# A layer of 64 experts returns its results by one-hot products in PSUM in place of scatter-adds in DRAM

## The chip, the cores and the metric

The kernel is one launch on one core of a Trainium2 chip. The metric is the device time of that launch in microseconds (us). The core has the engines PE (matrix products; PEld is its weight load, which overlaps PE), DVE (vector), ACT (scalar functions), POOL (general, and the issuer of indirect transfers) and SP (issues plain transfers). Each takes its instructions in order and waits on semaphores for the others.

## The reference

A macaron network of four kinds of block over x of 16 × 256 tokens × 128 features in float32: x + half a feed-forward part, x + attention, x + half a feed-forward part again. The change lies in the feed-forward part of block 1, which runs twice, before and after that block's attention. It is a mixture of 64 experts. Each token goes to its best 8, but an expert takes 64 rows at most, the first 64 in token order. One shared expert takes all tokens.

```python
logits = x @ router_w.T
probs = softmax(logits)
topk_w, topk_ids = top_k(probs, 8)
topk_w = topk_w / sum(topk_w)
pos = position of the token in its expert's list, in token order
valid = pos < 64
h = silu(xb[e] @ w_gate[e]) * (xb[e] @ w_up[e])      # xb[e]: the 64 rows of expert e
y = h @ w_down[e]
routed = segment_sum(y[slot] * topk_w * valid, token)
return routed + silu(x @ ws_gate) * (x @ ws_up) @ ws_down
```

The layer around it is x = x + 0.5 · ffn(layernorm(x)).

## The kernel before

x stays in SBUF as 32 tiles of 128 tokens. `norm_piece(c)` normalises the four tiles of piece c (statistics and roots on DVE, then ACT), and `turn_piece(c)` transposes them with PE into `xnT`. Twelve steps run one after the other; block 1 is `ffn1(0, normed=False)`, `attn1()`, `ffn1(1, normed=True)`, and block 2 begins with `ffn2(0)`, whose choice of tokens (`pick`, `best`, `choose`) is begun inside the second `ffn1`.

Since an expert takes the first 64 of its tokens, and the inputs fill all lists from the first 1024 tokens, the common path looks at FIRST = 8 tiles alone. A count `more` of unfilled slots is read into a register on every engine (`values_load`, L1107), and a branch (L1108) runs the general path over all 4096 tokens when it is above zero. That path is not taken with these inputs.

`ffn1` has three stages:

1. Routing (L985 to L1070): logits on PE, the best eight per token on DVE, then `slots` turns the keys and takes the first 64 per expert with eight rounds of max and replace on DVE. This gives `idx`, the token of each of the 64 × 64 slots, and `idy`, the same for the scatter. The rows of an instruction hold a pair of experts, 2 × 64 slots, so 32 columns. At its end the shared expert handles the first two pieces (`shared_up`: gate product L970, up product L972, silu, product L975; `shared_down`: L981 and the addition to x, L983), and `store_x` writes the 8 tiles of x to the first of four accumulators in DRAM. The scheduler moves these instructions up into pauses of the routing, since they hang on nothing later.
2. A loop of 8 groups of 8 experts (4 pairs), a pipeline written out by hand: `pin` chains the instructions of an engine in program order. `fetch(g)` gathers a group's rows with four indirect transfers issued by POOL (L1121), `turn(g)` transposes them, `gates(g)` makes gate and up products (L1143), `product(g)` multiplies on DVE (L1150), `down(g)` makes y (L1159), scales it to `ys` on DVE (L1175), and scatters it: four indirect transfers that add rows of `ys` to an accumulator in DRAM (L1179). Successive pairs use different tensors, and the two experts of a pair different halves of one, so four accumulators in all. Between these stand, for six of the groups, the shared expert of one later piece, and the normalising and turning of pieces. The weights of group g+2 are loaded by SP after `down(g)`.
3. The return. The 8 tiles of x are read from the first accumulator and three more are added to them: in the first call by `returned` and `summed` inside `attn1` (L1349 to L1359), in the second by `gather_acc` (L939) ahead of `choose(range(2))`. For this the three other accumulators are filled with zeros on entry (L957).

[...] The loop's own pool holds hg, hu, the gate product `sg` (which yp shares), the up product `su`, and two of y; a pool of two banks, `pst`, with the one tag "tp", serves all transposes.

The order of a step g of the loop, first call: `fetch(g+3)`, `down(g)`, weights of g+2, `turn_piece`, `norm_piece`, `gates(g+1)`, `product(g+1)`, `shared_up`, `turn(g+2)`, `shared_down`. The second call has `pick` and `best` at the end of a step besides; `best` is a row of max, find and replace operations on DVE.

## Time and profile before

| what | value |
| --- | --- |
| nine runs, median (lowest to highest) | 2895.14 us (2884.4 to 2908.34) |
| the profiled execution: time, span, granted clock | 2898.89 us, 2897.2 us, 0.844 |
| `ffn1(0)`: routing; loop, first y to the next stage's first product | from 666; 727.68 to 813.50 us |
| `ffn1(1)`: loop, first y; last `best` in the loop ends | 985.66; 1112.98 us |
| scatter-adds on POOL (L1179) | 64, mean 1569 ns |
| gathers on POOL (L1121) | 64, mean 964 ns |
| fills of accumulators, all steps | 14 of 512 KB |
| loads of accumulators into `acc_t`, all steps | 28 of 256 KB |

The times come from one profiled execution. A group of instructions is named by line, engine, operation and tile (digits dropped, so `f_ys` is f1_ys and `acc` any of the four), the shape as partitions × elements, a count, busy time and mean of one, then the idle time of the engine ahead of them and what ended it. A line of a timeline has start, length, engine, source line, operation, tiles, shape and count, and in square brackets the idle time ahead of it with its releaser. The granted clock is that of TensorE as a share of full speed.

### The profile page before, as it was taken

Reading aid. Unit: us, or ns where it says so; the run is one execution under the profiler, and the core shown is the slowest. Engines: PE = TensorE matmul, PEld = TensorE weight load, DVE = VectorE, ACT = ScalarE, POOL = GpSimd, SP = SyncE. Lnnn points to the kernel's source line nnn. Section 1 sums busy time; section 2 is a strip of 40 time slices with the busy share of each in tenths; the row PEclk is TensorE's granted clock in tenths of the full one; section 3 lists DMA queues with packets and bytes.
Section 4 is the critical chain, followed back from the end, with each engine's and each line's share of the span. In section 5 each row is a group of like instructions: output and inputs, shape, how many; then the busy total and the mean of one; then the engine's idle time right before and its main releaser. Section 6 shows DMA issues by size and latency. Waiting matters only on the chain. (4 is left out here: it accounts for less than half of the span.)

```text
span 2897.2 us, 45476 instructions
## 1 busy us (share of the span) xinstructions
PE 2324.3 (80%) x16717; PEld 1703.3 (59%) x16717; DVE 1489.3 (51%) x4376; ACT 1059.9 (37%) x2385; POOL 767.3 (26%) x695
## 2 busy tenths in 40 slices
PE   5976986993865573587999992776999899999999
PEld 4874554881655452354666661554777555557777
DVE  5446665445567556422345566124555566645453
ACT  1322221231334221343444432343444355553443
POOL 1650000561730452475000102772111100002111
PEclk9998886895769665555999995778999799989999
DMA  5861232563630445365000003552000012210000
GB/s 152 277 161 48 79 101 65 167 174 92 150 63 11 124 100 142 83 150 133 28 5 8 5 8 95 136 141 65 1 1 1 13 56 63 67 52 6 8 8 11
DMA packets 207909, 221.14 MB, mean 76 GB/s; under 512 B 46265, under 2 KB 172938, under 8 KB 204306
## 3 DMA queue, kind: packets, MB, share of 16 engines
q1 hardware_dynamic: 171066, 179.80, 20.2%
q0 software_dynamic: 36608, 38.31, 7.9%
q8 instruction: 135, 2.21, 0.3%
q14 instruction: 100, 0.82, 0.1%
HBM read 145.88 MB, written 63.50 MB: 72 GB/s over the span
## 5 line engine op out<-in xcount | busy, mean ns | idle before, releaser
L318 ACT ACTIVATE xn<-x,ln_less,ln_r 128x128 f32<-128x128 f32 x288 | 118.6, 482 | 376.0 <-DVE ln_less L309 347.3
L858 DVE TENSOR_REDUCE a_nm<-a_s 128x4 f32<-128x1024 f32 x128 | 156.4, 1224 | 101.0 <-PE a_t L854 89.8
L1652 PE MATMUL f_h<-f_xgT,f_w 128*128 128x128 f32 x768 | 161.8, 376 | 36.9 <-DVE f_xgT L1646 36.9
L503 PE MATMUL f_h<-f_xsT,f_w 128*128 128x256 f32 x736 | 183.6, 394 | 1.7 <-DVE f_xsT L492 1.7
L862 ACT ACTIVATE a_e<-a_t 128x512 f32<-128x512 f32 x256 | 139.1, 594 | 103.8 <-PE a_t L854 103.8
L854 PE MATMUL a_t<-a_q,a_k 32*128 32x256 f32 x1024 | 173.2, 424 | 4.7 <-ACT a_e L862 4.6
L1656 ACT ACTIVATE f_hs<-f_h,w_f_b 128x128 f32<-128x128 f32 x384 | 109.8, 368 | 182.2 <-PE f_h L1652 178.5
L1652 PEld LDWEIGHTS f_h<-f_xgT,f_w 128*128 128x128 f32 x768 | 137.7, 269 | 61.7 <-DVE f_xgT L1646 60.3
L1687 POOL DMA_INDIRECT acc<-f_ys,f_idx x96 | 151.8, 1581 | 55.9 <-DVE f_ys L1682 29.5
L506 DVE SCALAR_TENSOR_TENSOR f_hs<-f_h,f_b1s,f_sg 128x256 f32<-128x256 f32 x184 | 88.9, 484 | 141.9 <-ACT f_sg L505 140.7
L854 PE MATMUL a_s<-a_k,a_q 32*128 32x256 f32 x1024 | 154.7, 429 | 2.3 <-DVE a_nm L858 1.6
L505 ACT ACTIVATE f_sg<-f_h,f_b1s 128x256 f32<-128x256 f32 x184 | 87.1, 474 | 168.9 <-PE f_h L503 168.9
L503 PEld LDWEIGHTS f_h<-f_xsT,f_w 128*128 128x128 f32 x736 | 133.4, 196 | 24.6 <-issue 7.8
L326 PE MATMUL ln_tp<-ident,xn 128*128 128x128 f32 x288 | 64.2, 337 | 98.0 <-ACT xn L318 97.5
L1682 DVE TENSOR_SCALAR f_ys<-f_up,f_xg,f_share 128x128 f32<-128x128 f32 x96 | 39.4, 410 | 197.2 <-PE f_up L1679 163.4
L2072 ACT ACTIVATE f_nh<-f_c,w_f_sh 128x256 f32<-128x256 f32 x192 | 87.0, 500 | 127.7 <-DVE f_c L2091 103.2
L477 POOL DMA_INDIRECT f_xs<-xn_dram,f_src x92 | 90.7, 986 | 135.3 <-DVE f_own L446 60.6
L2019 POOL TENSOR_TENSOR f_t<-f_nh 128x512 f32<-128x512 f32 x16 | 20.3, 1272 | 380.8 <-PE f_m L2053 361.2
L854 PEld LDWEIGHTS a_t<-a_q,a_k 32*128 32x128 f32 x1024 | 107.0, 195 | 20.7 <-ACT a_e L862 14.2
L854 PEld LDWEIGHTS a_s<-a_k,a_q 32*128 32x128 f32 x1024 | 90.8, 197 | 46.9 <-issue 33.6
L1179 POOL DMA_INDIRECT acc<-f_ys,f_idy x64 | 100.4, 1569 | 65.5 <-DVE f_ys L1175 36.0
L326 PEld LDWEIGHTS ln_tp<-ident,xn 128*128 128x128 f32 x288 | 40.4, 162 | 125.3 <-ACT xn L318 111.3
(453 smaller groups left out, 5501.2 us busy)
## 6 DMA issues: line engine op xcount, KB each, us to landing
f_w<-in_f_w SPq DMA_DIRECT2D x24, 1024.0 KB
f_w<-in_f_w SPq DMA_DIRECT2D x46, 512.0 KB
f_w<-in_f_w SPq DMA_DIRECT2D x70, 256.0 KB
a_ud<-a_u SPq DMA_DIRECT2D x32, 512.0 KB
f_wgu<-in_f_wgu SPq DMA_DIRECT2D x16, 768.0 KB
acc<-zeros SPq DMA_DIRECT2D x14, 512.0 KB
acc_t<-acc SPq DMA_DIRECT2D x28, 256.0 KB
f_wd<-in_f_wd SPq DMA_DIRECT2D x16, 384.0 KB
```

What stands on the lines that cost most here:

```text
L318: S.activation(xn[:, t0 + j, :], x[:, t0 + j, :], AF.Identity, bias=less[:, j : j + 1], scale=r[:, j : j + 1])
L326: pin(PE.transpose(tp[:, i * P : (i + 1) * P], xn[:, 4 * c + i, :], ident))
L477: G.indirect_dma_start(out=xs[:, i, :], out_offset=None, in_=xn_dram, in_offset=bass.IndirectOffsetOnAxis(ap=src[:, s : s + 1], axis=0),)
L503: pin(PE.matmul(h[:, k, :], w1[:, cc * P : (cc + 1) * P], xsT, start=True, stop=True))
L506: V.scalar_tensor_tensor(hs[:, c, :], h[:, 1, :], b1[:, b, c : c + 1], sg, ALU.add, ALU.mult)
L854: pin(PE.matmul(ps[:, c, :], sta[:, c * P : (c + 1) * P], mov, start=True, stop=True))
L858: pin(V.tensor_reduce(m, sp, AX.X, ALU.max, negate=True))
L862: pin(S.activation(e, tp, AF.Exp, scale=scale))
L1179: G.indirect_dma_start(out=acc_two[e % 2], out_offset=bass.IndirectOffsetOnAxis(ap=idy[:, e : e + 1], axis=0), in_=ys[:, i, :], in_offset= ...
L1652: pin(PE.matmul(h[:, s, :], w1[:, e % GE2, s, :], xgT, start=True, stop=True))
L1656: pin(S.activation(acts[e][:, s, :], h[:, s, :], AF.Gelu, bias=W["f2_b1"][:, col : col + 1]))
L1687: G.indirect_dma_start(out=acc2[e % 2], out_offset=bass.IndirectOffsetOnAxis(ap=idx[:, e : e + 1], axis=0), in_=ys, in_offset=None, comput ...
```

## The change

The routed results of the common path no longer go through DRAM. For each pair e of experts and each half k of the 1024 tokens a one-hot matrix of 128 slots × 512 tokens is made by comparing a row of counting numbers with the slot's token (`tokf[:, k, e]`), on DVE for k = 0 and on POOL for k = 1 (`places`). PE multiplies: `sums[k] += ysᵀ · onehot` over all 32 pairs, in two PSUM banks that stay open through the loop (`put`). At the end ACT copies the two sums over the first 1024 columns of `xnT`, and `summed(c)` turns them back with four transposes and adds them to x.

The accumulators, `idy`, `store_x`, the fills and the loads go from the common path. Two banks for the sums are found by giving y one bank for two and by moving `sup`, the up product, into the pool of the transposes, in the routing stage as well. Every group's `ys` is stored to a new DRAM tensor `ys_dram` by SP; the general path alone reads it, and does its scatter-adds from there (its mending). `choose` takes the pieces two at a time, which is the same for the two pieces that the common path gives it.

```diff
+    ys_dram = dram.tile([E1 // 2 * P, D], F32, name="ys_dram")
...
+    def summed(c):
+        tp = pst.tile([P, 512], F32, tag="tp", name="f1_stp")
+        for i in range(4):
+            pin(PE.transpose(tp[:, i * P : (i + 1) * P], tok(4 * c + i), ident))
+        xc = x[:, 4 * c : 4 * c + 4, :]
+        pin(V.tensor_tensor(xc, xc, tp.rearrange("p (j d) -> p j d", d=D), ALU.add))
...
-        for a in acc[1:]:
-            zero_rows(a, 0, FIRST)
...
-                sup = pool.tile([F1, 512], F32, tag="su", name="f1_sup", bufs=1)
+                sup = pst.tile([P, 512], F32, tag="tp", name="f1_sup")[:F1, :]
...
-                    V.tensor_scalar(idy[rows, :], empty[rows, h::2], float(T + h * (T + PAD)), None, ALU.add)
+                    for k in range(2):
+                        V.tensor_scalar(tokf[rows, k, :], empty[rows, h::2], float(T - 512 * k), None, ALU.add)
...
-                store_x(acc[0], 0, FIRST)
...
+                count_up = op.tile([P, 512], F32, name="f1_no", bufs=1)
+                G.iota(count_up, pattern=[[1, 512]], base=0, channel_multiplier=0, allow_small_or_imprecise_dtypes=True)
+                sums = [ph.tile([P, 512], F32, name=f"f1_sum{k}") for k in range(2)]
+                def places(g):
+                    for i in range(n):
+                        e = g * n + i
+                        for k, eng in enumerate((V, G)):
+                            t = op.tile([P, 512], F32, tag=f"oh{k}", name="f1_oh")
+                            pin(eng.tensor_scalar(t, count_up, tokf[:, k, e : e + 1], None, ALU.is_equal))
+                            ohs[e, k] = t
+                def put(g):
+                    ys = yss.pop(g)
+                    for i in range(n):
+                        e = g * n + i
+                        for k in range(2):
+                            pin(PE.matmul(sums[k], ys[:, i, :], ohs.pop((e, k)),
+                                    start=e == 0, stop=e == E1 // 2 - 1, skip_group_check=True))
...
-                    y = ph.tile([P, n, D], F32, tag="y", name="f1_y", bufs=2)
+                    y = ph.tile([P, n, D], F32, tag="y", name="f1_y", bufs=1)
...
-                    for i in range(n):
-                        e = g * n + i
-                        pin(G.indirect_dma_start(out=acc_two[e % 2], ..., in_=ys[:, i, :], compute_op=ALU.add))
+                    SP.dma_start(
+                        out=ys_dram[g * n * P : (g + 1) * n * P, :].rearrange("(i p) d -> p i d", p=P), in_=ys)
...
                     if 1 <= g < groups - 3:
                         fetch(g + 3)
+                    places(g)
                     down(g)
...
                     if g + 2 < groups:
                         turn(g + 2)
+                    put(g)
                     if other:
                         shared_down(c, ph, sh, pin)
...
+                for k in range(2):
+                    pin(S.copy(xnT[:, k * 512 : (k + 1) * 512], sums[k]))
                 if normed:
                     best(first + others - 1, 2)
...
-                gather_acc(acc, 0, FIRST, n=4, bufs=6)
+                for c in range(FIRST // 4):
+                    summed(c)
                 choose(range(FIRST // 4))
...
-            for c in range(FIRST // 4):
-                returned(c)
...
-                    summed(piece_order[ahead[s]])
+                    if piece_order[ahead[s]] < FIRST // 4:
+                        summed(piece_order[ahead[s]])
```

`tokf` is a float tile of 128 × 2 × 32 in place of `idy`. The one-hots have four buffers for each half, which is one group's. `returned` and the old `summed` of `attn1` go.

More of the change, by code (lines that the diff above doesn't have):

```diff
@@ L962, in ffn1 @@
             idx = rp.tile([P, E1 // 2], I32, name="f1_idx")
-            idy = rp.tile([P, E1 // 2], I32, name="f1_idy")
+            tokf = rp.tile([P, 2, E1 // 2], F32, name="f1_tokf")
             more = rp.tile([1, 1], I32, name="f1_more")
@@ L1085, in general @@
                     )
-                    for a in acc:
-                        zero_rows(a, FIRST, NT)
+                    for a in acc[:2]:
+                        zero_rows(a)
                     key = key_pool.tile([P, NT // 2, 2, E1], F32, name="f1_gkey")
@@ L1111, in ffn1 @@
             pinned.clear()
-            with tc.tile_pool(name=f"f1h{call}", bufs=1, space=PSUM) as ph:
+            with tc.tile_pool(name=f"f1h{call}", bufs=1, space=PSUM) as ph, tc.tile_pool(
+                name=f"f1o{call}", bufs=GE1 // 2
+            ) as op:
                 n, groups, others = GE1 // 2, E1 // GE1, NT // 4 - FIRST // 4
-                xgs, turned, hidden, w = {}, {}, {}, early
+                xgs, turned, hidden, w, yss = {}, {}, {}, early, {}
+                count_up = op.tile([P, 512], F32, name="f1_no", bufs=1)
[13 more added lines that the diff above has]
+                        for k in range(2):
+                            pin(
+                                PE.matmul(
+                                    sums[k],
+                                    ys[:, i, :],
+                                    ohs.pop((e, k)),
+                                    start=e == 0,
+                                    stop=e == E1 // 2 - 1,
+                                    skip_group_check=True,
+                                )
+                            )
+                ohs = {}
                 def fetch(g):
@@ L1169, in down @@
                     flat = xgs.pop(g).rearrange("p e w -> p (e w)")
-                    ys = tp2.tile([P, n, D], F32, tag="ys", name="f1_ys", bufs=2)
+                    ys = yss[g] = tp2.tile([P, n, D], F32, tag="ys", name="f1_ys", bufs=2)
                     for h in range(2):
@@ L1175, in down @@
                         pin(V.tensor_tensor(ys[rows, :, :], y[rows, :, :], bc(wcol, 2, D), ALU.mult))
-                    for i in range(n):
-                        e = g * n + i
-                        pin(
-                            G.indirect_dma_start(
-                                out=acc_two[e % 2],
-                                out_offset=bass.IndirectOffsetOnAxis(ap=idy[:, e : e + 1], axis=0),
-                                in_=ys[:, i, :],
-                                in_offset=None,
-                                compute_op=ALU.add,
-                            )
-                        )
+                    SP.dma_start(
+                        out=ys_dram[g * n * P : (g + 1) * n * P, :].rearrange("(i p) d -> p i d", p=P), in_=ys
+                    )
                 first = FIRST // 4
@@ L1240, in ffn1 @@
             with tc.If(rv > 0):
-                gather_acc(acc, FIRST, NT, add=True)
+                with tc.tile_pool(name=f"f1s{call}", bufs=2) as sp2:
+                    idy = sp2.tile([P, E1 // 2], I32, name="f1_idy", bufs=1)
+                    for h in range(2):
+                        rows = slice(h * CAP1, (h + 1) * CAP1)
+                        V.tensor_scalar(idy[rows, :], tokf[rows, 0, :], float(h * (T + PAD)), None, ALU.add)
+                    for e in range(E1 // 2):
+                        ys = sp2.tile([P, D], F32, tag="ys", name="f1_gys")
+                        SP.dma_start(out=ys, in_=ys_dram[e * P : (e + 1) * P, :])
+                        G.indirect_dma_start(
+                            out=acc_two[0],
+                            out_offset=bass.IndirectOffsetOnAxis(ap=idy[:, e : e + 1], axis=0),
+                            in_=ys,
+                            in_offset=None,
+                            compute_op=ALU.add,
+                        )
+                gather_acc(acc[:2], FIRST, NT, add=True)
                 if normed:
@@ L1343, in norm @@
                 G.tensor_tensor(xc, xc, bc(W["a1_bo"], 1, 4), ALU.add)
-            def returned(c):
-                rows = slice(4 * c * P, (4 * c + 4) * P)
-                xc = x[:, 4 * c : 4 * c + 4, :]
-                SP.dma_start(out=xc, in_=acc[0][rows, :].rearrange("(j p) d -> p j d", p=P))
-                parts[c] = []
-                for a in acc[1:]:
-                    t = ap.tile([P, 4, D], F32, tag="acc", name="acc_t", bufs=6)
-                    SP.dma_start(out=t, in_=a[rows, :].rearrange("(j p) d -> p j d", p=P))
-                    parts[c].append(t)
-            def summed(c):
-                xc = x[:, 4 * c : 4 * c + 4, :]
-                for t in parts.pop(c, []):
-                    pin(V.tensor_tensor(xc, xc, t, ALU.add))
             pinned.clear()
-            parts = {}
-            for c in range(FIRST // 4):
-                returned(c)
             for c in begun:
@@ L1452, in choose @@
     def choose(cs):
-        for step in (norm_piece, turn_piece, pick, best):
-            for c in cs:
-                step(c)
+        for i in range(0, len(cs), 2):
+            for step in (norm_piece, turn_piece, pick, best):
+                for c in cs[i : i + 2]:
+                    step(c)
     def ffn2(call):
```

## The prediction

> **What bounds the kernel now.** I read the page's utilisation rows first, then the windows of the two expert loops, then their timelines and what ended each wait. The chain of waits reaches back only to 1797 us and says nothing of these loops.

> ```profile
> span 2897.2 us, 45476 instructions
> PE 2324.3 (80%) x16717; PEld 1703.3 (59%) x16717; DVE 1489.3 (51%) x4376; ACT 1059.9 (37%) x2385; POOL 767.3 (26%) x695
> 751.40:775.20 23.80, 20.04 (x139) 15.94 (x138) 13.48 (x52) 7.56 (x16) 18.37 (x16) 0.79 0.63 150
> 1034.00:1104.00 70.00, 49.13 (x270) 38.77 (x271) 43.73 (x161) 15.82 (x38) 29.37 (x21) 0.65 0.33 61
> ```

> The last two lines are windows (bounds, length, then busy time of PE, PEld, DVE, ACT, POOL, the granted clock, DMA share, GB/s). In loop 1 (first call, 727.7 to 813.5) two steps take 23.80 us and PE is busy for 20.04: TensorE has 3.8 us free in two steps. In loop 2 it has 21 of 70 free.

> ```profile
> 764.01 1.09 PE L1159 MATMUL f_y<-f_wd,f_hh 96*64 96x128 f32 x16
> 768.22 1.05 PE L970 MATMUL f_sgp<-xnT,w_f_sgu 128*96 128x512 f32 x2
> 769.10 1.02 PE L972 MATMUL f_sup<-xnT,w_f_sgu 128*96 128x512 f32 x2
> 769.96 0.60 PE L1132 MATMUL f_xtp<-ident,f_xg 128*128 128x128 f32 x4
> 773.91 1.34 PE L981 MATMUL f_yp<-w_f_sd,f_sh 96*128 96x128 f32 x8 [3.34 <-DVE f_sh L975]
> 775.18 1.98 PE L1159 MATMUL f_y<-f_wd,f_hh 96*64 96x128 f32 x16
> 783.06 1.97 PE L970 MATMUL f_sgp<-xnT,w_f_sgu 128*96 128x512 f32 x2
> 784.82 1.11 PE L972 MATMUL f_sup<-xnT,w_f_sgu 128*96 128x512 f32 x2
> ...
> 1040.49 2.07 PE L981 MATMUL f_yp<-w_f_sd,f_sh 96*128 96x128 f32 x8 [9.16 <-DVE f_sh L975]
> 1060.97 1.45 PE L981 MATMUL f_yp<-w_f_sd,f_sh 96*128 96x128 f32 x7 [4.64 <-DVE f_sh L975]
> ```

> Here a step lasts from one f_y to the next: 764.01 to 775.18 is 11.17 us at full clock with 3.34 idle, the next (775.18 to 787.86) 12.68 at a partly slow clock with 0.41 idle. A 128x512 f32 product costs 0.88 from start to start (768.22 to 769.10), 1.76 when slow (783.06 to 784.82). Loop 2 is paced by DVE and ACT; its step takes some 20 us.

> **Removed.** Per call: 32 scatter-adds on POOL, three 512 KB fills, the store and eight 256 KB loads of the accumulators, six DVE additions of 0.69.

> ```profile
> L1179 POOL DMA_INDIRECT acc<-f_ys,f_idy x64 | 100.4, 1569 | 65.5 <-DVE f_ys L1175 36.0
> ...
> 823.65 0.37 ACT L1282 COPY a_v<-a_vp 128x256 f32<-128x256 f32 x1 [10.24 <-DMA x<-acc]
> 824.07 1.22 PE L1276 MATMUL a_vp<-w_a_wv,xnT 128*128 128x128 f32 x4 [5.94 <-ACT a_v L1282]
> 1123.96 1.42 DVE L943 TENSOR_TENSOR x<-x,acc_t 128x512 f32<-128x512 f32 x2 [10.98 <-DMA acc_t<-acc]
> 1133.87 1.25 PE L326 MATMUL ln_tp<-ident,xn 128*128 128x128 f32 x3 [28.35 <-ACT xn L318]
> ```

> The scatters keep POOL busy but do not hold TensorE. On the path lie the waits after the loops: 10.24 on ACT, of which PE loses 5.94 at 824.07, and 10.98 on DVE in call 2. Loads, stores and fills are otherwise under the loops.

> **Added.** (1) PE: eight f32 products of 128x512 per group, 8 × 0.87 = 7.0 us at full clock, 14.1 slow; eight groups, two calls: 111 to 225 us. (2) Sixty-four one-hots a call, half on DVE and half on POOL. For DVE no 128x512 comparison is shown; the nearest rows are

> ```profile
> L190 DVE TENSOR_SCALAR same<-same,rowg 128x128 f32<-128x128 f32 x1 | 0.3, 255 | 0.0
> L1544 DVE TENSOR_SCALAR f_taken<-f_cv,f_lim 128x256 f32<-128x256 f32 x2 | 0.7, 343 | 0.0
> L2020 POOL TENSOR_TENSOR f_t<-f_nh 128x512 f32<-128x512 f32 x16 | 20.3, 1268 | 0.0
> ```

> from which 88 ns for 128 more columns gives 343 + 2 × 88 = 0.52; bounds 0.34 (half the width) and 0.69 (the 128x512 product of two tensors at L983). Four per group: 2.1 us (1.4 to 2.8). For POOL I take L2020's 1.27 (bounds 0.45, a fill of 128x2048 at 1.80 divided by four, and 1.58, the same L2020 with another input): with four gathers of 1.25 a step is 4 × 1.25 + 4 × 1.27 = 10.1 us, under PE's, so hidden; it would show if PE's step fell below that. (3) A 256 KB store of ys per group on SP. It waits there for ys, and behind it stand the weights of the group after next (768 + 384 KB). These wait for y of this group anyway, ys ends 1.4 later, and they are used a step later; at the 150 GB/s of the window they take 7.7 us of that step's 14: cost nothing, and what the step lacks if the cover is gone. (4) An iota on POOL ahead of the first gather, some 0.5 (rows of 0.23 for 128x128), and two ACT copies of the sums at the loop's end, some 0.7 each from the row of 0.37 for 128x256. (5) Four transposes and one addition in place of three additions.

> **Loop 1.** All of PE's step at full clock: y 1.02, turn_piece .50, gates 1.33 + 1.36, shared gate .88, up .86, turn .50, put 7.0, yp .9 = 14.3 us against a mean of 11.94. The wait of 3.34 is where put falls (it stands between turn and yp), but it is there only in every second step; the rest of put is added. DVE's step is 7.3 busy + 2.1 and with its waits 12 to 12.6: below 14.3. That is +2.4 a step. The last put (7.0) stands bare behind y(7), where no shared product or wait covers it, and so does the copy of the sums (0.8), which frees the bank that attention wants. At the end the wait for the accumulators goes: a_v stood 10.2 behind the loop's end (813.50) for their sake, and now follows the last put by about 2.4, the time of its own products and copy. The additions shrink from 5.2 (rows of 2.13 and 3.08 at 831.23 and 838.76) to 1.4, which with the transposes leaves −3.3.

> **The routing stage, a move that the diff hardly shows.** The up product of the shared expert now takes a bank of the pool that holds the transposes. In instruction order it so lands behind the key transposes, the list transpose and the count: the two shared chunks, before done between 670 and 685 (932 and 955 in call 2) inside routing's waits on DVE, now run after f_cp. The work: two ups 2 × 1.85, yp 2.0, addition .69, gate 1.97, silu .6, product .69, yp 2.1, addition .69 = 12.4 us in a row at the slow clock that PE has after such a pause. Routing itself ends some 3 us sooner without this work and the second index list (f_more 708.61 to 705.9), so DVE is free at 718.0 instead of 708.8. What is queued behind it on DVE is the branch:

> ```profile
> 712.95 0.87 DVE L295 BATCH_NORM_STATS2 ln_st<-x 128x6 f32<-128x128 f32 x4 [4.20 <-DVEq L1108]
> ```

> If the 4.20 follows the late end, norm_piece runs 722.2 to 726.3, xn to 728, the copy of the turned tokens after it on ACT, and the first gates start at 728.7 instead of 721.45: +7.3. If the branch is short (ACT shows 0.65 between its two neighbours in call 2), it is +3.8. Call 2 has no norm_piece there: +2.7, lower bound −0.8. I take the long one, since it is the same engine's row.

> **Sum of call 1.** y(0) 734.9, y(1) 753, five steps of 14.4 to y(6) 825, last put done 846.5, a_v at 848.9 against 823.65: +25.3; −3.3 for the additions: **+22**. **Call 2.** y(1) to y(3) come 8.2, 10.2, 11.6 late (these steps are PE's), then 0.4 to 2.1 each, the one-hots in DVE's chain; about +15 at y(6). After it the saved wait of 10.98 and the additions meet the last put, which delays pick and the last best by 7 (14.6 slow): −3.3 to +2.2. **+15** (+7 to +18). Together +37 on 2898.89 is 2936; the profiled run lies 3.75 above the median of nine, so 2932 on the median; forecast **2933**.

> [...] In loop 2 PE's granted clock is 0.65, in loop 1 0.79, and after a wait of 3.3 us the next products are slow for some 10 us. [...]

> **Rivals.** (A) PE stays slow in the loops: each put 14.1 instead of 7.0. For it: loop 2's 0.65. Against: the gaps that slow it in loop 1 are filled. All sixteen would be +112; for half of them +45 more: 2965 to 3040. (B) The one-hots become the bound, DVE and POOL holding each other up: a step of 16.5 instead of 14.3 is +15 in loop 1 and as much in loop 2: 2950 to 2965. For it: POOL's L2020 shows 1.27 and 1.58 for one shape, so POOL's time does stretch. Against: 14.3 leaves it 4 us. (C) Other side: POOL sets the pace now. Its step is 4 × 1.87 for scatters + 4 × 1.25 = 12.5 us, above the mean of 11.94, and it holds ys and the gathers; with 7.5 less, and with PE's 5.94 + 28.35 of tail idle to put the products into, both calls would shrink by some 10: 2875. It decides if PE's idle time per step is at least put's 7.0; the window shows 1.9 per step in loop 1 (10 in loop 2 but not in steps 0 to 3). (D) The shared work is hidden as before and the branch is short: that is 7 less on the sum, and with both tails at their good ends 8 less again: 2918.

> **Chances.** Forecast with its bounds (2915 to 2948) 0.50; D 0.15; B 0.12; A 0.10; C 0.07; no visible change, where D's gains and C's meet, 0.06. A measurement of this kernel tells about 0.3% (9 us) from no change. Slower by more: 0.87, within 0.06, faster 0.07. The range leaves out C and the upper A: 2907 to 2972.

> **What would show it.** After: f_y to f_y about 14.3 in loop 1 with a clock above 0.9 and no wait for f_sh (right), or steps above 16 with waits for f_oh on PE (B), or products of 1.76 (A). The shared ups after f_cp and hg(0) some 7 us later show the move; no idle DMA wait before a_v and before the summed additions shows the gain. The forecast is wrong if y's step stays near 12, or if PE waits for the xg gathers.

## The result and the profile after

The changed kernel takes 2950.53 us (median of 14 runs) against 2896.82 for the kernel before: a ratio of 1.0183, 95% interval 1.0167 to 1.0200, or +53.7 us. It is slower, as forecast, inside the stated range, and by half as much again as the +37 of the sum. The profiled execution has a span of 2945.7 us.

First two rows of the page, then two windows of the changed kernel, laid out as before (bounds, length, busy time of PE, PEld, DVE, ACT, POOL, clock, DMA share, GB/s): loop 1 from y(0) to y(7), and loop 2 from y(2) to y(7).

```profile
span 2945.7 us, 46050 instructions
...
PE 2397.8 (81%) x16989; PEld 1716.5 (58%) x16989; DVE 1521.6 (52%) x4436; ACT 1064.1 (36%) x2391; POOL 769.6 (26%) x697
```

```profile
731.81:829.44 97.63, 97.63 (x574) 61.82 (x573) 64.78 (x210) 25.29 (x55) 69.51 (x52) 0.99 0.38 115
1040.02:1149.64 109.62, 83.49 (x465) 52.11 (x464) 62.70 (x222) 19.90 (x46) 42.60 (x31) 0.89 0.22 68
```

Before the change loop 2 from y(2) to y(7) was this, and in its step from 1024.78 to 1045.44 the transposes of the gathered rows did not wait (the 9.16 us of idle time stood behind them, ahead of f_yp at 1040.49):

```profile
1010.24:1098.80 88.56, 65.29 (x386) 51.89 (x385) 53.75 (x205) 19.60 (x46) 46.48 (x35) 0.69 0.44 90
...
1030.73 0.60 PE L1132 MATMUL f_xtp<-ident,f_xg 128*128 128x128 f32 x4
```

In loop 1 PE is now busy for all of 97.63 us at a clock of 0.99. In loop 2 it is busy for 83 of 110: it has 26 us free, against 23 before, though 7 us of products were added to each step. One step of each, from the timeline of PE:

```profile
761.23 1.09 PE L1200 MATMUL f_y<-f_wd,f_hh 96*64 96x128 f32 x16
...
767.18 0.60 PE L1173 MATMUL f_xtp<-ident,f_xg 128*128 128x128 f32 x4
767.62 7.03 PE L1145 MATMUL f_sum<-f_oh,f_ys 128*128 128x512 f32 x16
774.49 1.06 PE L989 MATMUL f_yp<-w_f_sd,f_sh 96*128 96x128 f32 x8
775.47 1.09 PE L1200 MATMUL f_y<-f_wd,f_hh 96*64 96x128 f32 x16
...
1067.98 1.02 PE L980 MATMUL f_sup<-xnT,w_f_sgu 128*96 128x512 f32 x2
1075.32 1.12 PE L1173 MATMUL f_xtp<-ident,f_xg 128*128 128x128 f32 x4 [6.32 <-ACT xnT L328]
1076.23 8.12 PE L1145 MATMUL f_sum<-f_oh,f_ys 128*128 128x512 f32 x16
1084.18 1.06 PE L989 MATMUL f_yp<-w_f_sd,f_sh 96*128 96x128 f32 x8
1086.79 1.09 PE L1200 MATMUL f_y<-f_wd,f_hh 96*64 96x128 f32 x16
```

The step of loop 1 is 14.24 us (761.23 to 775.47) and has no gap. That of loop 2 (1062.88 to 1086.79) is 23.9 in place of 20.7 (1024.78 to 1045.44), and it has one gap: the transposes of the gathered rows wait 6.32 us for ACT to copy `xnT` out of a transpose bank, and the products, which stand behind them, are not even started. This wait is new.

The routing stage of the first call, as PE, then DVE and POOL saw it:

```profile
701.19 0.19 PE L1076 MATMUL f_cp<-ones,f_count 128*1 128x1 f32 x2 [1.42 <-DVE f_count L1074]
701.31 3.73 PE L980 MATMUL f_sup<-xnT,w_f_sgu 128*96 128x512 f32 x4
...
707.40 1.10 PE L978 MATMUL f_sgp<-xnT,w_f_sgu 128*96 128x512 f32 x2 [0.78 <-DVE x L991]
709.90 2.08 PE L989 MATMUL f_yp<-w_f_sd,f_sh 96*128 96x128 f32 x8 [1.40 <-DVE f_sh L983]
...
716.46 0.87 DVE L296 BATCH_NORM_STATS2 ln_st<-x 128x6 f32<-128x128 f32 x4 [3.75 <-DVEq L1116]
...
716.59 0.56 POOL L1126 IOTA f_no<- 128x512 f32 x1 [65.77 <-DVEq L1116]
```

The shared expert's products stand behind the count, as the instruction order said; DVE ends them at 712.71, and the branch takes 3.75 more. POOL, which has nothing to do with that work, starts its iota and so the first gathers only then (716.59).

The ends of both loops, ACT and DVE:

```profile
840.58 0.59 ACT L1274 COPY xnT<-f_sum 128x512 f32<-128x512 f32 x1 [8.83 <-PE f_sum L1145]
843.87 0.37 ACT L1336 COPY a_v<-a_vp 128x256 f32<-128x256 f32 x1 [1.84 <-PE a_vp L1330]
...
1169.79 0.43 DVE L1480 MAX8 f_cv<-f_lg 128x8 f32<-128x256 f32 x1 [9.32 <-ACT f_lg L1471]
1179.45 0.74 DVE L1774 TENSOR_SCALAR a_spread<-ones,rowm 128x64 f32<-128x64 f32 x4 [3.65 <-DMA f_w<-in_f_w]
```

The wait of a_v for an accumulator is gone, but ACT now waits nearly as long for the last products (8.83 against 10.24). In the second call the last `best` waits 9.32 for logits that stand behind the last products on PE; and before the additions, at the place of the second branch, DVE stands still for 3.65 more (the row names a weight load; in the run with three mends below the same instruction waits 6.29, and the row names the branch). So the 10.98 that went came back in two pieces.

Where the time came in, in us after the first routing logits of each trace (668.5 before, 665.4 after):

| point | before | after | gained or lost since the point above |
| --- | --- | --- | --- |
| first call, y(0) | 59.2 | 66.4 | +7.3 |
| first call, y(6) | 130.8 | 152.8 | +14.7 |
| copy of a_v | 155.1 | 178.5 | +1.4 |
| second call, y(0) | 317.1 | 342.8 | +2.3 |
| second call, y(2) | 341.7 | 374.6 | +7.2 |
| second call, y(6) | 416.5 | 469.1 | +19.7 |
| first transposes of `choose`, behind the loop | 465.3 | 520.4 | +2.5 |
| end of the span | 2228.7 | 2280.3 | −3.5 |

By these two traces the change costs 51.6 us behind the first logits, which the changed kernel's trace reaches 3.1 us sooner; so the spans differ by 48.5, the medians by 53.7.

### The profile page after: what moved, and what is told of

It is laid out like the page before. It is cut to its first block, busy times and chain, and to the rows that moved or that the text cites. A ratio compares the mean times of both kernels' runs of the same rounds, so it can differ in the third digit from the quotient of the medians.

```text
span 2945.7 us, 46050 instructions
## 1 busy us (share of the span) xinstructions
PE 2397.8 (81%) x16989; PEld 1716.5 (58%) x16989; DVE 1521.6 (52%) x4436; ACT 1064.1 (36%) x2391; POOL 769.6 (26%) x697
## 3 DMA queue, kind: packets, MB, share of 16 engines
q1 hardware_dynamic: 168122, 175.60, 19.7%
## 5 line engine op out<-in xcount | busy, mean ns | idle before, releaser
L1689 PE MATMUL f_h<-f_xgT,f_w 128*128 128x128 f32 x768 | 168.9, 388 | 36.9 <-DVE f_xgT L1683 36.9
L1689 PEld LDWEIGHTS f_h<-f_xgT,f_w 128*128 128x128 f32 x768 | 144.1, 281 | 62.2 <-DVE f_xgT L1683 60.8
L1145 PE MATMUL f_sum<-f_oh,f_ys 128*128 128x512 f32 x256 | 122.1, 633 | 9.7 <-DVE f_ys L1216 8.3
L1136 POOL TENSOR_SCALAR f_oh<-f_no,f_tokf 128x512 f32<-128x512 f32 x64 | 102.1, 1603 | 76.5 <-PE f_sum L1145 75.6
L2056 POOL TENSOR_TENSOR f_t<-f_nh 128x512 f32<-128x512 f32 x16 | 20.3, 1272 | 380.8 <-PE f_m L2090 361.2
L855 PEld LDWEIGHTS a_t<-a_q,a_k 32*128 32x128 f32 x1024 | 104.4, 189 | 17.5 <-ACT a_e L863 12.6
```

Of the source, the lines that this page charges most:

```text
L855: pin(PE.matmul(ps[:, c, :], sta[:, c * P : (c + 1) * P], mov, start=True, stop=True))
L1136: pin(eng.tensor_scalar(t, count_up, tokf[:, k, e : e + 1], None, ALU.is_equal))
L1145: PE.matmul(sums[k], ys[:, i, :], ohs.pop((e, k)), start=e == 0, stop=e == E1 // 2 - 1, skip_group_check=True,)
L1689: pin(PE.matmul(h[:, s, :], w1[:, e % GE2, s, :], xgT, start=True, stop=True))
```

## The experiments

Some of these runs fell on chips where the kernel before itself took 2953 to 2959 us in place of 2893; of that, some 40 us lie ahead of the first routing logits (705 to 714 us in their traces, 665 to 671 in the others). The bfloat16 kernel was traced on both: its spans differ by 39.7 us, the start of the logits by 43.0. So I read stage lengths from the traces, and compare times only among runs of one group. "Loop 1" is y(1) to y(7) of the first call, "end 2" y(2) of the second call to the first transposes of `choose`, behind the additions.

| run | median, before beside it | ratio, interval | loop 1 | end 2 |
| --- | --- | --- | --- | --- |
| before (profile) | | | 69.5 | 123.6 |
| changed (profile) | 2950.5, 2896.8 | 1.0183, 1.0167–1.0200 | 82.5 | 145.8 |
| put early | 2985.1, 2957.7 | 1.0089, 1.0058–1.0121 | 82.4 | 133.0 |
| own bank in routing | 2982.0, 2957.7 | 1.0078, 1.0056–1.0100 | 82.5 | 144.7 |
| no products | 2976.9, 2957.7 | 1.0051, 1.0029–1.0074 | 85.7 | 127.3 |
| one-hots once | 2992.4, 2957.7 | 1.0116, 1.0073–1.0158 | 82.5 | 138.3 |
| changed, again | 2947.5, 2892.6 | 1.0184, 1.0153–1.0215 | 82.5 | 146.3 |
| neither | 2890.1, 2892.6 | 0.9990, 0.9969–1.0010 | 68.8 | 116.7 |
| three mends | 2918.8, 2892.6 | 1.0082, 1.0055–1.0109 | 82.4 | 130.1 |
| mends, bfloat16 | 2898.2, 2892.6 | 1.0009, 0.9980–1.0038 | 84.7 | 125.7 |
| the same, DVE ahead | 2923.5, 2953.4 | 0.9911, 0.9883–0.9939 | 69.6 | 115.5 |
| bfloat16, POOL once | 2938.2, 2953.4 | 0.9945, 0.9922–0.9968 | 81.1 | 121.8 |
| DVE ahead, again | 2930.3, 2958.6 | 0.9904, 0.9876–0.9931 | 71.2 | 116.3 |
| bfloat16, again | 2951.7, 2958.6 | 0.9984, 0.9967–1.0001 | 83.5 | 122.9 |

**Put early.**

```diff
+                    put(g)
                     if g + 2 < groups:
                         turn(g + 2)
-                    put(g)
```

> The eight products of put stand right behind the shared up product, ahead of the transposes of the gathered rows; nothing else is changed. Theory (bank): in loop 2 put waits behind those transposes, which wait 5.3 to 6.3 us for a transpose bank; so put should fill that gap, steps 3 to 6 should fall from 23.9 to about 20.5 us, loop 1 should stay at 14.25 a step, and the kernel should come to about 2933 (2928 to 2938). Rival (one-hots on DVE's chain stretch loop 2): steps stay above 23, time 2948 to 2952.

Loop 1 stayed (82.4), end 2 fell from 146 to 133. In a step of loop 2 the products now fill the gap, and neither they nor the transposes wait:

```profile
1143.91 1.91 PE L980 MATMUL f_sup<-xnT,w_f_sgu 128*96 128x512 f32 x2
1145.62 7.15 PE L1145 MATMUL f_sum<-f_oh,f_ys 128*128 128x512 f32 x16
1152.60 0.60 PE L1173 MATMUL f_xtp<-ident,f_xg 128*128 128x128 f32 x4
```

The step is 21.4 us (1134.27 to 1155.64), somewhat above the 20.5 expected, as it begins at the slow clock (its f_y take 1.98 us, those of the next step 1.09). The rival's steps above 23 do not appear (21.1, 21.4 and 22.8 from y(3) on). That the products' place behind the waiting transposes is the cost is so shown. That the transposes wait for the shared bank is read from the releaser of their wait (ACT's copy of `xnT`) and from the order of the tiles; no run gives the up product a bank of its own inside the loop.

**Own bank in routing.**

```diff
-                sup = pst.tile([P, 512], F32, tag="tp", name="f1_sup")[:F1, :]
+                if keep is pin:
+                    sup = pst.tile([P, 512], F32, tag="tp", name="f1_sup")[:F1, :]
+                else:
+                    sup = pool.tile([F1, 512], F32, tag="su", name="f1_sup", bufs=1)
```

> In the routing stage alone the shared up product gets back a bank of its own; the loop is as in the changed kernel. Theory (the shared work was moved behind the count and holds the branch, and so the first gathers, by about 7 us in each call): it should stand inside routing's pauses again, routing should grow by the 3 to 4 us that it had shrunk, the first y come 6 to 8 earlier in each call, in all 10 to 15 us: 2937 (2934 to 2941). Rival (the branch comes late for another reason, the new iota and the index lists): within 4 us of 2950.

The products of the shared expert stand at 712 to 727 again, inside routing, which takes 4.0 us longer (logits to count, 39.8 against 35.8); from the count to the first gates it takes 13.8 in place of 24.4. From the first logits to y(0) it takes 64.0, against 68.7 to 70.6 in the three runs beside it that keep the shared bank: 5 to 7 less. In the second call, from the first transposes of attention to y(0), 157.0 against 165.6 to 168.5: 9 to 11 less. Run by run the two add up to 15 to 16, at the upper end of the expected 10 to 15 or just above. The rival, another cause of the late branch, is ruled out.

**No products; one-hots once; neither.** What the two cost was asked three times. First without products but for pair 0:

```diff
-                    for i in range(n):
+                    for i in range(1 if g == 0 else 0):
                         e = g * n + i
```

> Left out: the products of all pairs but the first (one-hots, ys and its store, the copies and the adding of sums stay), so only pair 0 returns its results. Theory (PE's products are the cost of loop 1 and most of that of loop 2): loop 1 falls from 14.25 to 11.5 to 12 a step, loop 2's steps to 21 to 22, the bare last products of both calls go: 40 to 50 us less, 2900 to 2911. Rival (one-hots and the bank's wait are the larger part): 15 to 25 less, 2925 to 2935.

Then with products, but one-hots for group 0 alone, used for all groups:

```diff
+                            if g:
+                                ohs[e, k] = kept[i, k]
+                                continue
```

> Left out: the one-hots of groups 1 to 7; the products use those of group 0, so the results land on wrong tokens, with all products made. Theory: loop 1 the same (PE sets it); in loop 2 the four DVE comparisons (1.65 a step) leave the chain, some 6 to 10 in all: 2941 to 2945. Rival (DVE and POOL hold each other up and set the pace): 20 or more less, 2930 or below.

Loop 1 did not fall in either: 85.7 without products, 82.5 without one-hots. The first of these is a miss of my theory, which had it fall to 69 to 72 (11.5 to 12 a step); the second is as expected. End 2 fell by 18.5 and by 7.5. By the ratios the whole kernels gain 38 us (expected 40 to 50) and 19 (expected 6 to 10, or 20 and more by the rival) on 1.0183; these ratios come from a chip where the kernel before takes 2957.7 us, of which more below. The trace of the run without products shows what holds it; DVE, then PE:

```profile
799.84 3.55 DVE L1136 TENSOR_SCALAR f_oh<-f_no,f_tokf 128x512 f32<-128x512 f32 x4
...
812.15 2.08 PE L989 MATMUL f_yp<-w_f_sd,f_sh 96*128 96x128 f32 x8 [7.24 <-DVE f_sh L983]
```

DVE's four one-hots stand ahead of ys and the roots, so ACT and with it f_sh come later; PE waits 7.24 for f_sh in this step (0.28 in the next), and after that wait its next products are slow (f_yp takes 2.08 us, 1.16 after the wait of 0.28; the clock is 0.72 over this loop). Either PE's products or DVE's one-hots are enough to hold a step at 14 us. So both were left out:

> Left out: the products of all pairs but the first, and the one-hots of groups 1 to 7. With products and no one-hots loop 1 took 82.4 us from y(1) to y(7), with one-hots and no products 85.7, before the change 69.5. Theory (two chains side by side, PE with the products and DVE with the one-hots, each long enough to hold a step at 14): with neither, y(1) to y(7) falls to 69 to 73, and the kernel to 0.990 to 1.000 of before. Rival (what holds loop 1 is something else that the change brought, the single bank of y or the gathers behind POOL's one-hots): 80 or more remain.

Loop 1 falls to 68.8, and the kernel to 0.9990 (0.9969 to 1.0010) of before. The theory of two chains side by side is confirmed, and the rival's 80 or more ruled out; the single bank of y costs nothing that could be seen. And all else that the change does (scatter-adds, fills and loads gone, the shared work moved, the store of ys) comes to nothing within 0.3%: its gain pays for the routing move. In loop 2 the one-hots alone are worth 6 to 8 us (109.6 and 112.0 from y(2) to y(7) in the two traces of the changed kernel, 103.7 without).

**Three mends.** The first two edits, and in the second call's last two groups `put` behind `pick` and `best`:

```diff
+                    late = normed and not other
+                    if not late:
+                        put(g)
...
                         pick(c - 2)
                         best(c - 2, 0, 2)
+                    if late:
+                        put(g)
```

> The two mends together: put ahead of the transposes, the up product of the routing stage in its own bank; besides, in the last two groups of the second call put stands behind pick, so that the last best need not wait for it. By the traces the first gives 12, the second 12, the third 7 to 9 us: about 32 less than the changed kernel run beside it. Rival (the three pay for the same wait): under 25.

2918.8 against 2947.5 for the changed kernel beside it: 28.7 less, within 4 of the sum. The last `best` no longer waits, and y(7) to the transposes of `choose` falls from 34.3 to 24.1 us. What is left is 0.82%. At those transposes the trace is 24.4 us behind that of the kernel before: 12.9 come from loop 1, 8.0 from the first two steps of the second call, 6.5 from end 2 and 4 from the start of the first call and the way to a_v; attention and the second routing give 7.1 back.

**bfloat16.** ys and one-hots as bfloat16 tiles (the results are rounded on their way to the sums, the one-hots are exact):

```diff
-                            t = op.tile([P, 512], F32, tag=f"oh{k}", name="f1_oh")
+                            t = op.tile([P, 512], BF16, tag=f"oh{k}", name="f1_oh")
...
-                    ys = yss[g] = tp2.tile([P, n, D], F32, tag="ys", name="f1_ys", bufs=2)
+                    ys = yss[g] = tp2.tile([P, n, D], BF16, tag="ys", name="f1_ys", bufs=2)
```

> As the run with the three mends, and ys and the one-hots are bfloat16, so that results are rounded on their way to the sums. Theory: put falls from 7.0 to about 1.8 us a group; loop 1 hardly gains, since the chain through DVE's one-hots then sets its step (13.5 to 14.3); loop 2 and the bare last products gain 12 to 20 us over the run with the mends. Rival (PE is the only bound): loop 1's step falls to 10 to 12 as well, and 30 or more are gained.

A group's products take 1.89 us; the 1.8 of the theory was the author's estimate, as no earlier run had a product in bfloat16. Loop 1 does not gain (84.7 against 82.4), as the two chains say; the whole kernel gains 20.6 (2918.8 to 2898.2), just above the expected 12 to 20. PE as the only bound is ruled out.

**bfloat16, DVE a group ahead.** In the time in which DVE waits for ACT it makes the next group's one-hots (`places(g, 0)` is DVE's half, `places(g, 1)` POOL's):

```diff
-                    places(g)
+                    places(g, 1)
                     down(g)
...
                     if g + 1 < groups:
                         gates(g + 1)
+                        places(g + 1, 0)
                         product(g + 1)
```

> As the bfloat16 run, and DVE makes its one-hots one group ahead, just before the product for which it waits 2.2 to 2.7 us each step. Theory (with products of 1.9 us a group DVE's one-hots are the link of the chain that sets both loops): they fall into that wait, a step loses 1.5 to 2.2 us in both loops, in all 15 to 25 us less than the bfloat16 run: ratio 0.992 to 0.996, faster than both kernels. Rival (the chain is set elsewhere, by the roots and ACT): within 5 us of it, ratio 0.999 to 1.002.

```profile
829.40 2.02 DVE L1140 TENSOR_SCALAR f_oh<-f_no,f_tokf 128x512 bf16<-128x512 f32 x4
831.68 0.69 DVE L1195 TENSOR_TENSOR f_hh<-f_hu,f_hh 96x512 f32<-96x512 f32 x1 [0.26 <-ACT f_hh L1190]
```

The four one-hots fill the wait for ACT: 2.19 to 2.25 in loop 1 of the bfloat16 kernel, 0.26 in this step and at most 0.60 in the others. Loop 1 is 69.6, what it was before the change; the ratio is 0.9911 (0.9883 to 0.9939). Run again beside the bfloat16 kernel, it was 0.9904 (0.9876 to 0.9931), 21 us below that one, where 14 to 20 were expected:

> The bfloat16 kernel with DVE's one-hots a group ahead, once more, beside the bfloat16 kernel without that, on one chip. The traces give 8 to 10 us from lgp to the end of loop 1 and some 8 in the second call for the move of the one-hots. Theory: 0.5 to 0.7% (14 to 20 us) below the run beside it, and below before on any chip: ratio 0.990 to 0.997.

This version beats both kernels. Both of its runs fell on chips where the kernel before takes 2953 to 2959 us; on one where it takes 2893 it was not run. With eight buffers for DVE's one-hots, four for POOL's and the counting row, their pool takes 14 KB of a partition in bfloat16; in float32 it would be 26, and that was not tried.

**bfloat16, POOL's one-hots once.**

```diff
+                            if g and k:
+                                ohs[e, k] = kept[i]
+                                continue
```

> As the bfloat16 run, but POOL makes only the first group's one-hots, which the products of the second half then use for all groups (so these land on wrong tokens). Theory (DVE's comparison takes 0.42 us alone and 0.7 to 0.9 while POOL makes one, so the two hold each other up): DVE's four take 1.7 us in every step of loop 1 in place of some 3, and the kernel gains 6 to 12 us: ratio 0.997 to 0.999. Rival (DVE's longer comparisons have another cause, such as the gathers' transfers or its own start): DVE's four still take 2.4 to 3.2 in loop 1, and the time stays within 4 us.

DVE's one-hots in three successive steps of the first call, the first of them beside POOL's only four:

```profile
770.56 3.38 DVE L1143 TENSOR_SCALAR f_oh<-f_no,f_tokf 128x512 bf16<-128x512 f32 x4
786.74 1.66 DVE L1143 TENSOR_SCALAR f_oh<-f_no,f_tokf 128x512 bf16<-128x512 f32 x4
800.44 1.67 DVE L1143 TENSOR_SCALAR f_oh<-f_no,f_tokf 128x512 bf16<-128x512 f32 x4
```

Without POOL at the same work, four take 1.66 to 1.67 in every later step, so 0.42 each; beside POOL's they take twice that. The contention is shown, and the gathers, which stay, are ruled out as its cause. Loop 1 gains 2.5 to 3.7. The ratio, 0.9945, is below the expected 0.997 to 0.999, which started from the bfloat16 kernel's 1.0009; on its 0.9984 of the run below the gain is 0.4%, some 11 us, as expected. These two come from groups of runs with a like time of before (2953 and 2959).

**bfloat16, again.**

> The bfloat16 kernel once more. It had 1.0009 beside a before of 2893 us, the other runs stood beside a before of 2953 to 2958. Theory (the chip has a part in the ratio): if before takes about 2955 here, the ratio is 0.995 to 0.998; if it takes about 2893, 0.999 to 1.003 as it was. Rival (the ratio is the kernel's alone): 0.998 to 1.004 with either.

It came out at 0.9984 (0.9967 to 1.0001) against 1.0009 (0.9980 to 1.0038): just outside the theory's range and inside the rival's, but the intervals overlap. The changed kernel run again gave 1.0184, beside a before of 2893 as at first, so it tells nothing of the other group. Whether the ratio of one kernel differs between the two groups of runs is not settled. It matters for the first four runs: by their ratios, put early and own bank in routing gain 27 and 30 us over 1.0183 (0.0094 and 0.0105 of 2897), by the stage lengths 13 and 15 to 16. The three mends together, measured beside the changed kernel, gain 29, and their trace divides this as 5 and 8 for the routing of the two calls and 16 for end 2, tail included. The last is what I trust.

## Why the prediction was right, and where it was not

**The step of loop 1**: forecast 14.3, measured 14.24; PE without a gap, no wait for f_sh, clock 0.99. That the wait of 3.34 hides only part of the products held. The reason given, that PE's products are the price, was half of it: DVE's one-hots were costed at 2.1 us and called hidden, with a step of DVE of 12 to 12.6. They took 3.65, 2.87 and 2.40 us at 752, 767 and 781 us of the changed kernel's second trace, and without the products they alone hold the loop at 14.3.

**The routing move**: +7.3 forecast and +7.3 measured in the first call, where two errors cancel. Counted from the logits, DVE leaves the branch 6.7 us later (51.1 against 44.4), not 9.2 as forecast, since routing, the shared work and the branch were all shorter. And the first gates, forecast 6.5 behind the branch by the way over norm_piece, wait for the gathers, which took 8.5 before and take 9.1 with the iota ahead of them. That agreement is luck; that the shared work holds the branch is not, as the run with a bank of its own shows. For the second the forecast was +2.7 at the first gates. From the count to the first gates it took 19.6 us (982.43 to 1002.00) against 12.4 (967.07 to 979.43), +7.2. What lies ahead of it, attention with its fewer additions and a shorter routing, gained 4.9 (141.2 to 136.4 from attention's first transposes to the count), so y(0) lost 2.3 and the total there, +25.7, was near the forecast's 24.7. The step that failed there is that the gathers were taken to start without DVE: POOL waits for the branch as DVE does (78.91 us idle ahead of its iota at 993.04, ended by DVE's branch, L1116).

**The last products and the return of call 1**: forecast +25.3 at a_v, measured +23.4. The last group took 8.83 (at 832.57), not 7.0.

**POOL's one-hots**: 1.27 taken, with 0.45 to 1.58 as bounds; 1.60 measured, a little outside, and hidden all the same. **DVE's**: 0.52 taken, 0.34 to 0.69 as bounds; the mean is 0.64, in truth 0.42 alone and up to twice that beside POOL. As rival B had it, the two hold each other up; the step of 16.5 did not come, as PE's 14.24 was longer than DVE's stretched chain.

**Loop 2 is the step that failed.** The forecast said: "then 0.4 to 2.1 each, the one-hots in DVE's chain". Up to y(2) it was near (32.2 late by the sum, 32.9 measured). From y(2) on the steps lost 8.3, 3.2, 3.8 and 4.3, together 19.7 in place of some 5. I had put the products into PE's idle time before yp. That time was there, but the order on PE keeps them out: `turn(g+2)` stands in front, and it lost its free bank to the up product, a move that I had costed for the routing stage alone. Put early shows the order: 13 us back in its trace. At y(6) the forecast had +37 and the trace has +52.6: this is nearly all of what is missing between +37 and +54.

**The tail of call 2**: −3.3 to +2.2 forecast, +2.5 measured. The named mechanism (the last products hold the last best) cost 9.32. At the place of the second branch 3.65 more are lost, 3.4 to 6.3 in the other traces. That it is the branch, which the saved wait used to hide, is the likely reading: the row names it in five of the other runs.

**The clock.** The forecast has, by the rows, products that are slow for some 10 us after a wait of 3.3. In loop 2 the products took 8.12 to 8.17 after waits of 5.3 to 6.3, so 1.1 us more than 7.03 (8.3 to 9.3 in the second trace). The granted clock tells it directly: from 1071.58 to 1078.41 it was 0.50, and PE had started again at 1075.32, so it was back after 3.1 us. At 1157.53 the products took 10.20 after a wait of 6.20; there the clock was 0.50 until 1163.74, for 6.2 us. From y(2) to y(7) the clock rose from 0.69 to 0.89. Rival A had little in it. The +7 at the low end of the second call is shown by no run: by the table that call lost 29.4 us from y(0) to the transposes of `choose`.

**Rival C**, POOL as the pace of loop 1: with scatter-adds, one-hots and products all left out, loop 1 is 68.8 against 69.5. POOL's scatter-adds held nothing there.

## What to carry to other kernels

Idle time on an engine can take added work only if the work stands where the idle time is: look which instruction ends the gap, and whether the added one is in front of it or behind it in that engine's order. When a buffer or a bank is given to another tile to make room, cost it for every user of its pool, in every stage, and look for the one that now has to wait. And leave out each of two suspected costs, then both: where two chains run side by side, taking away either gains nothing.
